# Bias loads on GpSimd's queue, a later request for the second tokens, a new order of the first norms, and another home for the residual, in a transformer block on one core

## The chip, the cores and the metric

The kernel runs on one core of one Trainium2 chip. The metric is the device time of one execution in microseconds (us), lower is better. A core has five engines that each work through their own queue of instructions in order: TensorE (PE in the profile; its weight loads are listed as PEld), VectorE (DVE), ScalarE (ACT), GpSimd (POOL) and SyncE (SP), which here only asks for DMA transfers. Engines wait for each other, and for transfers, through semaphores.

## The reference, cut to what matters

The input is 2048 tokens of 1024 features, all float32. The block is a layer norm and attention with a residual, then a layer norm and a gated feed-forward net with a residual:

```python
x = x + attn(layernorm(x), wq, bq, wk, bk, wv, bv)   # wl is not used for the result
x = x + ffn(layernorm(x), w1, w2, w3)

# attn: q, k, v = h @ w.T + b, seen as (token, 32 heads, 32);
scores  = einsum("bshd,bstd->bsht", q, k) / sqrt(32)  # 32 x 32 for each token: heads against heads
context = einsum("bsht,bstd->bshd", softmax(scores), v)

# ffn: w1, w2 (2752 x 1024) and w3 (1024 x 2752) are first quantized to 16 levels and back,
# in blocks of 64 that are scaled by the block's largest magnitude
y = (silu(h @ dq1.T) * (h @ dq2.T)) @ dq3.T
```

## The kernel before, in words

**Tiling.** Tokens lie in 16 tiles of 128. The three projections work on pairs of tiles, p = 0 to 7. Two token tiles by two halves of the features make a matrix of 2 by 2 blocks, and the weights are cut into 2 by 2 blocks too, so a pair's product is made with seven block products in place of eight (`products`, L352). Their left sides are the four blocks A11, A12, A21, A22 and four sums of these (`three` L398, `fourth` L403); their right sides are B11, B12, B21, B22 and four differences T1 to T4. The seven products come in a written order: B11, T3, T2, B21, T1, B22, T4. After the second and each later one `fill(n)` is called, with n = 7, 6, 2, 5, 3, 4 in turn, and does other work.

**Sweeps.** Three sweeps over the pairs follow each other: queries, keys, values. In the queries' sweep the tokens are loaded (`load_x` L458), normed (`normed` L329: statistics on VectorE, the power of -1/2 on GpSimd, the subtraction and scaling on VectorE), transposed on TensorE for the next pair (L486, four transposes into one PSUM tile `pt`, four such tiles per pair, three `pt` buffers), and copied out twice by ScalarE: L489 into A for the queries and keys, L490 into V, with another order of the tokens, for the values. Both A and V are stored to DRAM and read again in the later sweeps. The weights' differences T1 to T4 for queries are made once at the start (L519 to L534, L570); those for keys and values are made in eight chunks (`weight_chunk` L538), one per pair, and stored. A pair ends with `qk_T` (L411), which turns the two results to heads and adds the bias. The keys' sweep makes the scores and the softmax beside its products; the values' sweep makes the context, adds it to the tokens (`residual` L684), stores the sum to DRAM (x1d, L693), norms it (L337) and transposes it for the feed-forward part (`keep_T` L723), with four differences (L745) that go to DRAM through buffers `xU`.

**Background.** A generator, `background` (L219), works on the feed-forward weights all along: load a block of weights, take the largest magnitudes (`absmax` L200, with 16 small multiplications on ScalarE at L195), then 15 steps that build the level of each element. Twelve of these steps are a pair of a ScalarE instruction (L242, into one of two buffers `sg`) and a VectorE instruction (L243), which reads it. Another 16 multiplications at L195 (or one at L254 later) undo the scale. `advance(n)` takes n steps of the generator; `finish` (L147) transposes a finished block on TensorE (`ptw`, L161), copies it out (L162) and stores it (wd, L180). `scaled` (L192) is what issues the rows at L195.

**Feed-forward part.** From about 783 us on, gate and up products run with seven products again (`Unit` L912), and the down products are copied out at L1037 and added into x1d in DRAM by GpSimd's accumulating DMAs (L1039).

**What sets the order.** TensorE's instructions run as written (L283). For the other engines a planner orders what is ready, so a step of the background can be put before or behind a copy that TensorE needs. `tc.issue_after(i)` puts what it encloses behind i in the queue of i's own engine; it is an order of issue and no wait for i's end. SyncE asks for the transfers in the planner's order, and a request waits there until its own conditions hold, with all behind it.

**The opening.** SyncE asks for token tile 0 in two halves and tile 1, then for the weight blocks B11, B22, the one that becomes T1, and B21 (L503 to L508). ScalarE asks for the three biases in four pieces each (L509, `load_bias` L323). TensorE does 16 transposes of the identity. VectorE makes the statistics of tile 0, those of tile 1, and then both norms; their GpSimd parts are kept in order through `opening`. The first products follow; the second tiles (2 and 3) are loaded at the top of the loop (L564).

Of the kernel before, what the change touches and what calls it, by code (L numbers as in the profile page):

```python
# [12 lines left out]
FP = mybir.dt.float32  # L13
AF = mybir.ActivationFunctionType
ALU = mybir.AluOpType
# [3 lines left out]
P = 128  # L19
# [50 lines left out]
def preln_block_kernel(  # L70
# [39 lines left out]
    fs = ctx.enter_context(tc.tile_pool(name="fs", bufs=2))  # L110
    hook = {"scale": "ACT"}

    def mean_var(pool, src, dst):
        st = pool.tile([P, 2, 6], FP, tag="st", name="st")
        for j in range(2):
            nc.vector.bn_stats(st[:, j, :], src[:, ts(j, 512)])
        nc.vector.bn_aggr(dst, st.rearrange("p a b -> p (a b)"))
# [73 lines left out]

    def scaled(dst, src, by, nb):  # L192

        for n in range(nb):
            nc.scalar.mul(dst[:, ts(n, BLOCK)], src[:, ts(n, BLOCK)], by[:, n : n + 1])  # L195

    def width(kind, c):
        return KC * min(P, F - c * P) if kind == "3" else E
# [61 lines left out]
    def advance(n):  # L260
        for _ in range(n):
            next(bg, None)
# [57 lines left out]
        src = block(m, *RAW[name]) if name in RAW else wtD[m, int(name[1])]  # L320
        nc.sync.dma_start(new_w(name), src)

    def load_bias(b, nm):  # L323
        t = wpool.tile([P, 32], FP, tag=nm, name=nm)
        for g in range(4):
            nc.scalar.dma_start(t[g * 32 : (g + 1) * 32, :], b)
        return t

    def normed(src, dst, order=None):  # L329
        mv = small.tile([P, 2], FP, tag="mv", name="mv")  # L330
        rs = small.tile([P, 1], FP, tag="rs", name="rs")
        mean_var(small, src, mv)
        with tc.issue_after(order["last"]) if order else nullcontext():
            order_end = inv_std(rs, mv[:, 1:2])
        if order is not None:
            order["last"] = order_end.ins
        done = nc.vector.tensor_scalar(dst, src, mv[:, 0:1], rs, ALU.subtract, ALU.mult)  # L337
        hook["normed"] = done.ins
        return dst
# [114 lines left out]
    ps_t = sweep.enter_context(tc.tile_pool(name="ps_t", bufs=3, space=PSUM, side="right"))  # L454

    xt = {}

    def load_x(i):  # L458
        xt[i] = work.tile([P, E], FP, tag="x", name="xt", bufs=2)
        for n in range(2 if i == 0 else 1):  # L460
            cols = ts(n, TB) if i == 0 else slice(None)
            nc.sync.dma_start(xt[i][:, cols], xf[ts(i, P), cols])

    opening = {}

    def normed_x(i):
        xn = work.tile([P, E], FP, tag="xn", name="xn", bufs=2)
        return normed(xt.pop(i), xn, opening if i < 2 else None)

    class Inputs:  # L470

# [10 lines left out]
        def transposes(self, j):  # L482
            for half in range(2):
                pt = ps_t.tile([P, 4, P], FP, tag="pt", name="pt")
                for k in range(4):
                    nc.tensor.transpose(pt[:, k, :], self.xn[j][:, ts(4 * half + k, P)], ident)  # L486
                n = (SA11, SA12, SA21, SA22)[2 * j + half]
                a, v = (self.a21, self.v21) if n == SA21 else (self.A[:, n], self.V[:, n])
                nc.scalar.copy(a, pt)  # L489
                nc.scalar.copy(  # L490
                    v.rearrange("p k (c m) -> p k c m", c=4),
                    pt.rearrange("p k (m c) -> p k c m", c=4),
                )

        def finished(self):
# [10 lines left out]
    load_W("q", "B22")  # L506
    nc.sync.dma_start(new_w("T1"), block("q", 0, 1))
    load_W("q", "B21")  # L508
    qb_sb, kb_sb, vb_sb = (load_bias(b, nm) for b, nm in ((qb, "qb"), (kb, "kb"), (vb, "vb")))  # L509

    warm = ps_t.tile([P, 4, P], FP, tag="pt", name="warm")
    for _ in range(16):
# [3 lines left out]
    nxt.transposes(1)  # L516
    b12 = W["T1"]
    new_w("T3"), new_w("T2"), new_w("T4")
    with tc.issue_after(three(nxt.A, nxt.a21).ins):  # L519
        for n in range(2):  # L520
            k = slice(2 * n, 2 * n + 2)
            t3 = nc.vector.tensor_tensor(  # L522
                W["T3"][:, k], W["B22"][:, k], b12[:, k], ALU.subtract
            )
# [35 lines left out]
    for p in range(NP):  # L560
        more = p + 1 < NP
        now = nxt
        if more:
            load_x(2 * p + 2)  # L564
            load_x(2 * p + 3)
            with nullcontext() if p else tc.issue_after(opened):
                nxt = Inputs(p + 1)
            if p == 0:
                with tc.issue_after(hook["normed"]):
                    nc.vector.tensor_tensor(W["T4"], W["B21"], W["T2"], ALU.subtract)  # L570

        def fill(n):
            if n in (7, 3):
                flush(1)
            if n == 5 and more:
                nxt.transposes(0)
                nxt.transposes(1)
            with nullcontext() if p else tc.issue_after(opened):
                advance(0 if n == 5 else 1)

        cs = products(now.A, fill, (lambda name: None) if more else next_W("k"), ps_t)
        flush(1)
        if more:
            nxt.finished()
        for j in range(2):
            t = work.tile([P, 32, NH], FP, tag="qd", name="qd", bufs=2)
            qk_T(t, cs[j], qb_sb)
            nc.sync.dma_start(qD[2 * p + j], t)
        with nullcontext() if p else tc.issue_after(opened):
            now.finished_v()  # L590
        weight_chunk("kv"[p // 4], p % 4)
        advance(2)
        if p == NP - 2:
            first = load_A(opD, 0)
    sweep.close()


    sweep, sweep_at = ExitStack(), ExitStack()
    work = sweep.enter_context(
        tc.tile_pool(name="workk", bufs=1, side="right", reuse_waits="tile")  # L600
# [83 lines left out]
    def residual(i, at, x1):  # L684

        cx = work.tile([P, E], FP, tag="cx", name="cx")
        nc.vector.transpose(
            cx.rearrange("p (h d) -> p d h", d=D),
            at[:, :, 0:256].rearrange("p c (s d) -> p d s c", d=D),
        )  # L690
        nc.vector.tensor_tensor(x1, x1, cx, ALU.add)
        for n in range(2):
            nc.sync.dma_start(x1d[i][n], x1[:, ts(n, TB)])  # L693
        return normed(x1, x1)

    ops = {}

# [25 lines left out]
    def keep_T(i, x1n):  # L723

        t = work.tile([P, 2, 4, P], FP, tag=f"xT{i % 2}", name="xT")
        for half in range(2):
            pt = bank("pt").rearrange("p (k t) -> p k t", t=P)
            for k in range(4):
                nc.tensor.transpose(pt[:, k, :], x1n[:, ts(4 * half + k, P)], ident)
            nc.scalar.copy(t[:, half], pt)  # L730
        cols = ts(i // 2 % 4, P)
        tbp = i // 8
        names = ("B11", "B21") if i % 2 == 0 else ("B12", "B22")
        for n in range(2):
            nc.sync.dma_start(xd[names[n], tbp][:, :, cols], t[:, n])
        if i % 2 == 0:
            even["t"] = t
            return
        b11, b21 = even["t"][:, 0], even["t"][:, 1]
        b12, b22 = t[:, 0], t[:, 1]  # L740
        u = {}
        for n in range(4):
            u[n + 1] = work.tile([P, 4, P], FP, tag="xU", name="xU", bufs=2)
            y, z = ((b12, b11), (b22, u.get(1)), (b22, b12), (b21, u.get(2)))[n]
            nc.vector.tensor_tensor(u[n + 1], y, z, ALU.subtract)  # L745
            nc.sync.dma_start(xd[f"T{n + 1}", tbp][:, :, cols], u[n + 1])
# [464 lines left out]
```

## Time and profile before

| | us |
|---|---|
| median of three runs | 2480.15 |
| lowest, highest | 2476.73, 2480.97 |
| the profiled execution | 2484.77 |
| its span, first to last instruction | 2483.0 |
| TensorE busy | 2389.2 (96% of the span) |
| VectorE busy | 1981.2 (80%) |
| ScalarE busy | 1610.2 (65%) |
| GpSimd busy | 278.4 (11%) |

The queries' sweep takes the span's first 240 us or so, the keys' goes to about 537, the values' to about 783. The page lists busy times, the groups of instructions by line, and who waited for whom. "Idle before" is the time that an engine stood still before a row, and the arrow names what ended it. Line numbers (L489) are those of the kernel before. A busy TensorE is not TensorE at its best: its granted clock, a column of the tables by stretches, is 0.5 in ten stretches of 3.4 or 6.8 us before 820 us, and 1.0 in most others.

### The profile page before, as it was taken

Reading aid. Unit: us, or ns where it says so; the run is one execution under the profiler, and the core shown is the slowest. Engines: PE = TensorE matmul, PEld = TensorE weight load, DVE = VectorE, ACT = ScalarE, POOL = GpSimd, SP = SyncE. Lnnn points to the kernel's source line nnn. Section 1 sums busy time; section 2 is a strip of 40 time slices with the busy share of each in tenths; the row PEclk is TensorE's granted clock in tenths of the full one; section 3 lists DMA queues with packets and bytes.
Section 4 is the critical chain, followed back from the end, with each engine's and each line's share of the span. In section 5 each row is a group of like instructions: output and inputs, shape, how many; then the busy total and the mean of one; then the engine's idle time right before and its main releaser. Section 6 shows DMA issues by size and latency. Waiting matters only on the chain.

```text
span 2483.0 us, 36752 instructions
## 1 busy us (share of the span) xinstructions
PE 2389.2 (96%) x14000; PEld 1117.1 (45%) x14000; DVE 1981.2 (80%) x2211; ACT 1610.2 (65%) x3267; POOL 278.4 (11%) x352
## 2 busy tenths in 40 slices
PE   7999999999899999999999999999999999999998
PEld 4444455545445444444444444444444444444433
DVE  8999688879988597889989899898998988871022
ACT  3566544344554278898887888889889798881200
POOL 0010000000000012030120301203012030020300
PEclk9999999999999999999999999999999999999999
DMA  8888543666669588384883948739577394872983
GB/s 310 301 295 339 214 154 125 228 221 216 198 234 317 196 299 172 126 183 156 310 186 114 185 163 289 181 140 183 165 280 173 132 206 159 278 159 88 173 310 122
DMA packets 179745, 513.90 MB, mean 207 GB/s; under 512 B 16176, under 2 KB 70448, under 8 KB 157168
## 3 DMA queue, kind: packets, MB, share of 16 engines
q1 hardware_dynamic: 138672, 438.08, 48.5%
q0 software_dynamic: 40320, 73.42, 18.4%
q8 instruction: 110, 1.80, 0.3%
q14 instruction: 67, 0.55, 0.1%
q10 hardware_dynamic: 576, 0.05, 0.0%
HBM read 283.69 MB, written 227.80 MB: 206 GB/s over the span
## 4 chain that ended last, share of the span: by engine, by line
issue 25%; ACT 13%; DVE 13%; PE 11%; DMA 6%; POOL 1%; DVEq 0%; POOLq 0%; ACTq 0%
DVE r L243 8%; DMA x1d<-acc 5%; ACT sg L242 4%; PE z L343 4%; ACT wn L195 4%; ACT acc L1037 2%; ACT r L195 2%; PE z L1024 2%; PE q L343 2%; PE po L1104 1%; POOL x1d L1039 1%; PE po L1115 1%; PE y L1024 1%; PE rr L343 1%; ACT wop L162 1%
## 5 line engine op out<-in xcount | busy, mean ns | idle before, releaser
L243 DVE SCALAR_TENSOR_TENSOR r<-sg,r 128x1024 f32<-128x1024 f32 x780 | 945.3, 1213 | 104.1 <-ACT sg L242 72.7
L242 ACT ACTIVATE sg<-wn 128x1024 f32<-128x1024 f32 x780 | 812.6, 1053 | 309.6 <-DVE r L243 294.0
L1039 POOL DMA_DIRECT2D x1d<-acc x280 | 243.0, 887 | 1282.1 <-ACT acc L1037 1138.4
L343 PE MATMUL z<-xB,w 128*128 128x512 f32 x720 | 324.6, 599 | 5.6 <-ACT u L944 3.8
L343 PE MATMUL z<-xT,w 128*128 128x512 f32 x656 | 298.1, 597 | 4.6 <-ACT u L937 4.3
L343 PE MATMUL q<-xT,w 128*128 128x512 f32 x656 | 291.6, 592 | 0.0
L195 ACT ACTIVATE wn<-wn,rc 128x64 f32<-128x64 f32 x1032 | 267.5, 341 | 19.1 <-DVE rc L215 19.1
L1024 PE MATMUL z<-w,h 128*128 128x512 f32 x496 | 233.6, 599 | 9.4 <-ACT acc L1037 6.5
L343 PEld LDWEIGHTS z<-xB,w 128*128 128x128 f32 x720 | 134.6, 191 | 173.6 <-issue 153.0
L343 PEld LDWEIGHTS z<-xT,w 128*128 128x128 f32 x656 | 122.4, 191 | 154.4 <-issue 137.0
L343 PEld LDWEIGHTS q<-xT,w 128*128 128x128 f32 x656 | 123.3, 190 | 149.5 <-issue 146.9
L343 PE MATMUL z<-wT,A 128*128 128x512 f32 x384 | 178.2, 607 | 2.9 <-ACT g L362 2.5
L343 PE MATMUL q<-wT,A 128*128 128x512 f32 x384 | 174.5, 598 | 2.5 <-DVE wT L522 2.5
L343 PE MATMUL z<-wB,A 128*128 128x512 f32 x320 | 153.9, 626 | 12.8 <-ACT u L362 12.8
L195 ACT ACTIVATE r<-r,am 128x64 f32<-128x64 f32 x608 | 154.8, 342 | 14.6 <-DVE r L243 14.3
L1024 PE MATMUL y<-w,h 128*128 128x512 f32 x320 | 150.4, 594 | 1.3 <-DVE h L1003 1.1
L343 PE MATMUL rr<-xB,w 128*128 128x512 f32 x328 | 147.5, 592 | 0.0
L1024 PEld LDWEIGHTS z<-w,h 128*128 128x128 f32 x496 | 92.1, 191 | 121.7 <-issue 96.7
L207 DVE TENSOR_REDUCE am<-wn 128x16 f32<-128x1024 f32 (+1 forms) x65 | 78.3, 1204 | 54.5 <-ACT r L195 54.2
L1037 ACT COPY acc<-z 128x512 f32<-128x512 f32 x160 | 92.9, 580 | 36.9 <-PE z L1024 26.3
L343 PEld LDWEIGHTS q<-wT,A 128*128 128x128 f32 x384 | 72.6, 192 | 90.5 <-issue 85.4
L343 PEld LDWEIGHTS z<-wT,A 128*128 128x128 f32 x384 | 71.5, 193 | 83.0 <-issue 78.1
(132 smaller groups left out, 2585.8 us busy)
## 6 DMA issues: line engine op xcount, KB each, us to landing
x1d<-acc POOLq DMA_DIRECT2D x280, 256.0 KB, 6.4
wd<-wop SPq DMA_DIRECT2D x31, 2048.0 KB, 7.5
w<-wd SPq DMA_DIRECT2D x41, 1280.0 KB, 7.8
wn<-in_w_dram SPq DMA_DIRECT2D x63, 512.0 KB, 5.0
xT<-xdT SPq DMA_DIRECT2D x28, 1024.0 KB, 9.2
xB<-xdB SPq DMA_DIRECT2D x24, 1024.0 KB, 9.0
w<-wd SPq DMA_DIRECT2D x42, 512.0 KB, 5.0
w<-wd SPq DMA_DIRECT2D x10, 1536.0 KB, 7.6
```

What stands on the lines that cost most here:

```text
L162: nc.scalar.copy(o[:q, first + half], pt[:q])
L195: nc.scalar.mul(dst[:, ts(n, BLOCK)], src[:, ts(n, BLOCK)], by[:, n : n + 1])
L207: nc.vector.tensor_reduce(am[:, :nb], v.rearrange("p (b e) -> p b e", e=BLOCK), AX.X, ALU.max, apply_absolute_value=True,)
L242: nc.scalar.activation(t, v, AF.Copy, bias=-edge * by, scale=by)
L243: nc.vector.scalar_tensor_tensor(r, t, code, r, ALU.min, ALU.max)
L343: nc.tensor.matmul(dst, w[:, k, :], xop[:, k, :], start=start and k == 0, stop=stop and k == 3, skip_group_check=True,)
L1024: nc.tensor.matmul(dst, side[n][:, ts(q, P)], w3T[g[2 * m]][:, W3[n]], start=start and m == 0, stop=stop and m == 1, skip_group_check=True,)
L1037: nc.scalar.copy(t, src)
L1039: nc.gpsimd.dma_start(x1d[8 * tbp + 2 * q + j][n], t, accum_op=ALU.add)
L1104: nc.tensor.matmul(po, hs[c][j][:, ts(q, P)], w3T[c][:, ts(n, 512)], start=(c == g[0]), stop=False, skip_group_check=True,)
L1115: nc.tensor.matmul(po, hs[NFULL][r, ts(q, P)], w3T[NFULL][r, ts(n, 512)], start=False, stop=True, skip_group_check=True,)
```

## The change: the order of the opening, the queue of the biases, and three buffers

- The twelve bias requests move from ScalarE's queue to GpSimd's. They stand behind the GpSimd part of tile 1's norm. The bias of the queries gets its buffer in the sweep's own pool.
- All of tile 1's norm on VectorE, statistics too, is queued behind the norm of tile 0.
- The request for tile 2 on SyncE now waits until `three` has ended on VectorE for the first pair (`opening["first"]`).
- In the queries' sweep, the small multiplications of `scaled` are queued on ScalarE behind the last copy into V that was written before them (`marked`, `behind`).
- In the first pair, `fill` takes no step of the background at n = 7, 6 and 2; these three steps come later.
- In `residual`, the sum of tokens and context is written over the context (`cx`, one buffer), stored from there, and the norm is written to `x1`. Before, the sum was written over the tokens, stored from there and normed in place.
- `xU` gets three buffers in place of two.

```diff
+    urgent = {"last": None, "rule": ()}
+
+    def marked(ins):
+        urgent["last"] = ins.ins
+
+    def behind(kind):
+        last = urgent["last"]
+        return tc.issue_after(last) if last and kind in urgent["rule"] else nullcontext()
...
     def scaled(dst, src, by, nb):
-        for n in range(nb):
-            nc.scalar.mul(dst[:, ts(n, BLOCK)], src[:, ts(n, BLOCK)], by[:, n : n + 1])
+        with behind("scale"):
+            for n in range(nb):
+                nc.scalar.mul(dst[:, ts(n, BLOCK)], src[:, ts(n, BLOCK)], by[:, n : n + 1])
...
-    def load_bias(b, nm):
-        t = wpool.tile([P, 32], FP, tag=nm, name=nm)
+    def load_bias(b, nm, pool):
+        t = pool.tile([P, 32], FP, tag=nm, name=nm)
         for g in range(4):
-            nc.scalar.dma_start(t[g * 32 : (g + 1) * 32, :], b)
+            nc.gpsimd.dma_start(t[g * 32 : (g + 1) * 32, :], b)
...
+    urgent["rule"] = ("scale",)          # back to () after the queries' sweep
...
-            nc.sync.dma_start(xt[i][:, cols], xf[ts(i, P), cols])
+            load = nc.sync.dma_start(xt[i][:, cols], xf[ts(i, P), cols])
+        if i == 2:
+            tc.add_manual_dep(
+                load.ins,
+                opening["first"].name,
+                mybir.DependencyInfo(
+                    mybir.DependencyClass.Sync, mybir.DependencyReason.DATA
+                ),
+                reason="the first weights come first",
+            )
...
-        return normed(xt.pop(i), xn, opening if i < 2 else None)
+        with tc.issue_after(hook["normed"]) if i == 1 else nullcontext():
+            return normed(xt.pop(i), xn, opening if i < 2 else None)
...
-                nc.scalar.copy(
-                    v.rearrange("p k (c m) -> p k c m", c=4),
-                    pt.rearrange("p k (m c) -> p k c m", c=4),
+                marked(
+                    nc.scalar.copy(
+                        v.rearrange("p k (c m) -> p k c m", c=4),
+                        pt.rearrange("p k (m c) -> p k c m", c=4),
+                    )
                 )
...
-    qb_sb, kb_sb, vb_sb = (load_bias(b, nm) for b, nm in ((qb, "qb"), (kb, "kb"), (vb, "vb")))
...
-    with tc.issue_after(three(nxt.A, nxt.a21).ins):
+    with tc.issue_after(opening["last"]):
+        qb_sb = load_bias(qb, "qb", work)
+        kb_sb = load_bias(kb, "kb", wpool)
+        vb_sb = load_bias(vb, "vb", wpool)
+    opening["first"] = three(nxt.A, nxt.a21).ins
+    with tc.issue_after(opening["first"]):
...
-                advance(0 if n == 5 else 1)
+                advance(0 if n == 5 or p == 0 and n in (7, 6, 2) else 1)
...
-        nc.vector.tensor_tensor(x1, x1, cx, ALU.add)
+        nc.vector.tensor_tensor(cx, x1, cx, ALU.add)
         for n in range(2):
-            nc.sync.dma_start(x1d[i][n], x1[:, ts(n, TB)])
-        return normed(x1, x1)
+            nc.sync.dma_start(x1d[i][n], cx[:, ts(n, TB)])
+        return normed(cx, x1)
...
-            u[n + 1] = work.tile([P, 4, P], FP, tag="xU", name="xU", bufs=2)
+            u[n + 1] = work.tile([P, 4, P], FP, tag="xU", name="xU", bufs=3)
```

More of the change, by code (lines that the diff above doesn't have):

```diff
@@ L595, in preln_block_kernel @@
     sweep.close()
+    urgent["rule"] = ()
     sweep, sweep_at = ExitStack(), ExitStack()
```

## The prediction, written before the changed kernel ran

> **What bounds the kernel now.** I read the page's busy times first, then the table by stretches over the first 240 us (the queries' sweep, where most edits lie), then who waited for whom, then the timeline around the longest waits.
>
> ```profile
> PE 2389.2 (96%) x14000; PEld 1117.1 (45%) x14000; DVE 1981.2 (80%) x2211; ACT 1610.2 (65%) x3267; POOL 278.4 (11%) x352
> ```
>
> TensorE is busy for 96%, so what can be won is its 94 us of idle time and the time at half clock. In the next view the columns are busy time and count of PE, PEld, DVE, ACT and POOL, then TensorE's granted clock, then the DMA engines' share and GB/s.
>
> ```profile
> 12.00:18.98 6.98, 4.47 (x12) 1.92 (x10) 3.36 (x5) 2.65 (x6) 0.00 (x0) 1.00 1.03 388
> 18.98:34.50 15.52, 15.52 (x32) 6.73 (x33) 15.07 (x20) 1.17 (x2) 1.48 (x4) 0.89 0.96 364
> 34.50:42.00 7.50, 1.49 (x13) 1.23 (x11) 7.12 (x12) 7.29 (x23) 0.00 (x0) 0.91 0.67 274
> 42.00:48.60 6.60, 6.57 (x12) 3.31 (x13) 6.60 (x9) 6.16 (x9) 0.00 (x0) 0.58 0.91 305
> 60.00:220.10 160.10, 152.35 (x432) 72.86 (x431) 155.02 (x215) 93.15 (x202) 13.81 (x20) 0.99 0.80 299
> 220.10:240.00 19.90, 19.90 (x49) 8.80 (x48) 19.43 (x23) 12.91 (x27) 0.00 (x0) 1.00 0.94 369
> ```
>
> Two things stand here. Up to 48.6 us TensorE loses 8.5 us by idling (2.5 and 6.0), and its clock is 0.50 for 20.2:23.6 and 40.7:47.5, where 10.2 us do 5.1 us of work. From 60 to 220 us VectorE is busy for 155 of 160 us: it has hardly more room than TensorE. Who TensorE waited for in the first 300 us (total, times, longest):
>
> ```profile
> PE pt L486 <- ACT V L490: 12.4, 4, 6.0
> PE q L343 <- DVE wT L522: 2.5, 1, 2.5
> PE z L343 <- ACT g L362: 2.5, 1, 2.5
> ```
>
> And on ScalarE's timeline, where the longest of these comes from:
>
> ```profile
> 34.71 0.59 ACT L362 COPY u<-z 128x512 f32<-128x512 f32 x1 [6.28 <-PE z L343]
> 35.19 3.93 ACT L195 ACTIVATE wn<-wn,rc 128x64 f32<-128x64 f32 x16
> 39.02 0.57 ACT L489 COPY A<-pt 128x512 f32<-128x512 f32 x1
> ...
> 41.39 0.59 ACT L490 COPY V<-pt 128x512 f32<-128x512 f32 x1
> ```
>
> Sixteen background scales stand between TensorE's transposes and the copies that free their PSUM tile. SyncE's own waits in the first 60 us:
>
> ```profile
> SPq L321 <- DMA wB<-in_wqT_dram: 3.5, 1, 3.5
> SPq L321 <- DMA kb<-in_kb_dram: 2.7, 1, 2.7
> SPq L321 <- DMA qb<-in_qb_dram: 1.8, 1, 1.8
> ```
>
> The weight requests were held back 8.0 us in all: the biases take turns at the same completion semaphores, so B11, asked for at 3.94, waited for a bias to land. T1's block, asked for at 7.47, landed at 17.6, and VectorE's first subtraction began at 17.70 after 2.67 us of idling.
>
> **The change part by part, the opening.** Without the biases all seven requests can be issued in a row (0.45 us each, by 4 us). Transfers land in order of request, T1's after 4 MB. At the 388 GB/s of 12.00:18.98 that is 10.8 us, from 2.0 us on: 12.8 us. At the 257 GB/s seen before 12 us it is 18.3 us, no gain. I take 13 to 14, since the row at 388 is the one in which biases are nearly gone. Then the next to be late is `three`: tile 0's norm moves from 8.09 to about 6.2, but tile 1's statistics (6.64) now wait for it, so tile 1's norm stays near 9.6. ScalarE is rid of twelve issues that kept it until 8.06, so its copies of tile 0 end some 2 us earlier, those of tile 1 about 0.9, and `three` ends near 14.4 in place of 15.03. T3's halves (1.18 each) are ready by 16.8, as TensorE ends B11's product (16.47). The idle 2.51 and the half clock after it (3.4 us, 1.7 lost) go; T2's second half, four subtractions of 1.2 later, costs back up to 0.3. Transposes of tiles 2 and 3: 34.51 less 3.9, about 30.6. Tile 2's request waits for `three`: asked for at 14.4 in place of 11.97, but two weight loads (0.5 MB each) pass it, so it lands at 19 to 21, where it landed at 21.6; nobody waits, since VectorE takes it up only after T2 (21.6 or so).
>
> The biases cost GpSimd 12 issues. The nearest row is L1039, 862 ns (up to 1218): 10.3 to 14.6 us from 9.5 on, so 20 to 24; GpSimd's next norm part is due at about 23.5. Ends: 0 and +1 us; I take 0, since the first user of a bias, L414, comes at 52.97. A rule of the Trainium skill speaks against this edit: SBUF — State Buffer, "A bandwidth-pool intuition that's wrong (but worth ruling out)", says a request that GpSimd issues, about 0.62 us alone, takes about 3.1 us beside a VectorE copy that holds the shared port. By that the twelve would end at 47 us and hold tile 2's norm by over 20. L1039 ran at 862 ns with VectorE busy for most of the time, so the sum goes by the row.
>
> **First pair's transposes.** The three skipped steps include the only one that puts L195 there. In the built order ScalarE now runs u4's copy and at once A, A, A21, V21, so the fourth transposes wait only for four copies, as at 72 us, where the wait was 1.36. The first pair ends earlier by 3.9, plus 6.04 - 1.36 = 4.7, plus the half clock 3.4: about 12 us, its last product at 40 in place of 52.07. There VectorE is late next. Its instructions up to that pair's L394 lose 8.4 us by median durations, most of it six code steps, and it begins T3 some 3 us earlier; as it then waits for ScalarE's copies, I put L394 at 42.5 for 52.38.
>
> **Pairs two to seven.** The skipped steps come back here. In the built order of VectorE, 45 code steps lie ahead of the seventh L394 (220.1 us) where 47 did, so over these six pairs VectorE has four steps more, 5 us, and was full. Its whole work to that point falls by 2.6 us by median durations; idle time that can go is 2.7 in the opening and up to 5 in 60:220. So the gain there is 2.6 + 2.7 = 5.3 to 10.3, whatever TensorE could do; I take 7. TensorE's own waits there hardly change: five of the six pairs now have the order A, A, A21, V21 (7 us), where the waits for V and AV without the first made 12.4 + 1.4 - 6.0 = 7.8. So VectorE decides.
>
> **Keys.** No edit here, but the background is out of step with the products: in the first two pairs 2.46 and 1.09 us of waits for ScalarE's copies and 6.8 us at clock 0.50 (3.4 lost) can vanish. In the built order 17 scales and a sign step precede the first u4, so I take half: -3; ends 0 and -7.
>
> **Values.** VectorE's waits from 530 to 870 us:
>
> ```profile
> DVE xU L745 <- DMA xdT<-xU: 11.2, 6, 4.0
> DVE x L337 <- DMA x1d<-x: 11.1, 5, 5.7
> ```
>
> The norm no longer waits for its own store, and the third `xU` takes most of the other. `cx` must now wait for the store before it is written again: pairs of stores and the next L687 lie 3 to 6 us apart at the tightest (stored by 767 to 768, written at 771.0), so 0 to +2. But who waited for VectorE? TensorE's longest waits there are for u4:
>
> ```profile
> 617.70 0.57 ACT L362 COPY u<-z 128x512 f32<-128x512 f32 x1
> 624.29 1.06 ACT L242 ACTIVATE sg<-wn 128x1024 f32<-128x1024 f32 x1 [6.03 <-DVE r L243]
> ...
> 627.91 0.57 ACT L362 COPY u<-z 128x512 f32<-128x512 f32 x1
> ```
>
> Three sign steps stand ahead of the copy and each needs VectorE to free `sg`. In the built order three pairs of the values' sweep still have this (sign steps between u2 and u4: 3, 4 and 3; before 3, 2 and 3, which cost 4.27, 3.29 and 4.13). What can go are the waits after 770 us, 8 us with three stretches at half clock (5.1 lost). I take -3 of these 13; ends +6 (one u4 stall more, 4.3 and 1.7 of clock) and -9.
>
> **Feed-forward part.** Its waits (some 30 us, 11.8 for `acc`) are a matter of where the background's rows fall; the built order has as many rows ahead of the critical copies as before. 0, with +-4.
>
> Sum: -7 - 3 - 3 = -13. The profiled execution took 2484.77 (span 2483.0), so 2471.8; it stood 4.6 above the median of the runs, so the median becomes 2467.
>
> **Rivals.** A: VectorE takes it back. If passes two to seven are as full as 155 of 160 says and the u4 copies there wait for sign steps, the first pair's 12 us shrink to 3, and keys and values shift without a gain: 2477. For it: 99.03 us busy in 100:200. Against it: the 2.7 us in the opening are VectorE's own.
>
> B, slower: the pattern at 617 us in the queries' sweep. There u4 stands ahead of the transposes' copies, and in the built order pairs two to seven all have two to four sign steps between u2 and u4, while VectorE is full. At 4.3 and 1.7 us each, less the 1.4 already counted, that is 4.6 a pair: all six cost 28 and end at 2495. It decides from four pairs on (18.4, more than 13 + 5). Against it: 100.67 had three sign steps and cost 2.59 with no loss of clock.
>
> C, more: the idle and half-clock stretches of keys and values after 260 us go too: -7 and -9 with -9 for queries, 2455.
>
> D: T1's block lands late anyway (18 us): the opening's 3.9 stay away, VectorE's gain falls to 3, sum -9: 2471, inside the forecast.
>
> **How the numbers follow.** Forecast (D with it) 0.55, own range 2460 to 2474; C 0.17; A 0.14; B 0.14. What a measurement can tell from no change is 0.2%, 5 us: under 2475.2 is faster, over 2485.1 slower. Faster is forecast and C, 0.72; same is A, 0.14; slower is B, 0.14. The range 2453 to 2484 takes in C and A and leaves B out.
>
> **What would show it.** T1's subtraction begins by 15 us with no wait over 1 us; no clock of 0.50 from 20 to 48 us; L195 after the copies into V; the first pair's L394 near 42.5 and the seventh's near 213; no L337 wait for a store. I am wrong if T1 still lands after 17 us, if GpSimd's issues take 3 us each and tile 2's norm is late, or if TensorE's waits for L362 and L490 in 50:220 exceed 15 us.

## The result, and the profile after

The changed kernel takes 2501.42 us (median of five runs, 2500.15 to 2504.92), the kernel before 2480.97 in the same comparison (2476.73 to 2483.29): a ratio of 1.0084, with the interval 1.0072 to 1.0097. It is slower, where 2467 was forecast. Its profiled execution took 2503.82 us (span 2502.0), 19.0 more than the span before; the medians lie 20.5 apart.

The changed kernel's lines are those of before plus 11 or 12 near the top (L180 is L191, L343 is L355, L362 is L374, L195 is L207), plus 23 or 24 in the queries (L486 is L509, L490 is L514), plus 30 further down (L818 is L848, L1024 is L1054). First the busy times on the page of the changed kernel:

```profile
PE 2388.8 (95%) x14000; PEld 1115.6 (45%) x14000; DVE 1984.7 (79%) x2211; ACT 1612.9 (64%) x3267; POOL 282.1 (11%) x364
```

No engine is busy for more than 3.7 us longer than before, and TensorE's busy time is the same within 0.4 us: the 19 us are idle time of TensorE (113.2 us for 93.8). The table by stretches (busy time and count of PE, PEld, DVE, ACT and POOL, then TensorE's clock, the DMA share and GB/s) shows that the queries' sweep, which the prediction looked at most, did get better:

```profile
8.00:12.00 4.00, 0.87 (x5) 0.79 (x5) 2.12 (x4) 1.76 (x4) 2.50 (x5) 0.53 1.04 382
12.00:18.98 6.98, 6.68 (x17) 3.34 (x16) 4.42 (x6) 2.64 (x5) 4.62 (x10) 0.78 1.06 389
18.98:34.50 15.52, 14.67 (x43) 6.62 (x41) 15.06 (x22) 2.94 (x6) 1.49 (x4) 1.00 0.98 375
60.00:220.10 160.10, 148.61 (x421) 71.10 (x419) 155.53 (x214) 92.90 (x202) 10.69 (x20) 0.98 0.80 303
```

The half clock from 20 to 24 us has gone, and so has that from 41 to 47. The one in 8 to 15 us is not new: in the kernel before, the 16 transposes at 8.90 us took 3.67 us, 0.23 each, where twelve at 34.51 took 1.47, 0.12 each, so TensorE was at half pace there too, although its row says 1.00; and before_late (an experiment below), whose opening is that of before, shows 0.50 from 7.6 to 14.4. From 60 to 220 us VectorE is as full as before. The first pair's copies now stand as predicted, with the scales (L207) behind them, in the timeline of the changed kernel:

```profile
32.73 0.59 ACT L374 COPY u<-z 128x512 f32<-128x512 f32 x1 [6.28 <-PE z L355]
33.21 1.57 ACT L512 COPY A<-pt 128x512 f32<-128x512 f32 x3
34.64 0.63 ACT L514 COPY V<-pt 128x512 f32<-128x512 f32 x1
...
43.93 3.94 ACT L207 ACTIVATE wn<-wn,rc 128x64 f32<-128x64 f32 x16
```

The loss is elsewhere. From 780 us on, who TensorE waited for (total, times, longest), in the changed kernel:

```profile
PE z L1054 <- ACT acc L1067: 13.8, 13, 2.3
PE z L1054 <- DMA w<-wd: 9.2, 1, 9.2
```

and in the kernel before, the same rows:

```profile
PE z L1024 <- ACT acc L1037: 11.8, 11, 2.2
...
PE z L1024 <- DMA w<-wd: 2.9, 1, 2.9
```

The second row is one event: TensorE needs the last large block of quantized w3, number 18, which the background has made and stored (L191) and SyncE loads again (L848). In the changed kernel's timeline:

```profile
2157.73 0.32 SPq L191 DMA_DIRECT2D wd<-wop  x1
2166.46 0.32 SPq L848 DMA_DIRECT2D w<-wd  x1
2172.49 4.43 PE L1054 MATMUL z<-w,h 128*128 128x512 f32 x6 [9.22 <-DMA w<-wd]
```

and before:

```profile
2140.39 0.32 SPq L180 DMA_DIRECT2D wd<-wop  x1
2148.81 0.32 SPq L818 DMA_DIRECT2D w<-wd  x1
2152.61 3.77 PE L1024 MATMUL z<-w,h 128*128 128x512 f32 x5 [2.90 <-DMA w<-wd]
```

The store is issued 17.3 us later, though TensorE was only 12.7 us behind at the last mark ahead of it (unit 35 in the count below). The block's load then landed 6.0 us after it was asked for, in place of 3.8; two other loads (L839, L840) had been asked for about 4 us ahead of it, but that they slowed it was not tested.

Where the 19.0 us came in, at marks on TensorE that both traces have (the start of a pair's last product, T4; in a feed-forward unit the start of its product with B21; units are counted from 1):

| mark | before, us | after, difference | in this stage |
|---|---|---|---|
| first pair of the queries | 48.6 | -9.4 | -9.4 |
| last pair of the queries | 240.3 | -4.4 | +5.0 |
| second pair of the keys | 301.7 | -1.0 | +3.4 |
| last pair of the keys | 497.4 | +0.7 | +1.7 |
| last pair of the values | 777.8 | +3.7 | +3.0 |
| first feed-forward unit | 842.5 | +6.5 | +2.8 |
| unit 32 | 2052.1 | +12.5 | +6.0 |
| unit 36 | 2211.4 | +20.3 | +7.8 |
| end | 2483.0 | +19.0 | -1.3 |

Such marks of single executions scatter by 2 to 3 us, as runs show in which nothing was edited up to a mark. The keys' last products end near 501 us; the 537 us given above for the end of the keys is the end of the values' first pair, in which the last scores are still made.

### The profile page after: what moved, and what is told of

It reads as the page before. It is cut to its first block, busy times and chain, and to the rows that moved or that the text cites. A ratio compares the mean times of both kernels' runs of the same rounds, so it can differ in the third digit from the quotient of the medians.

```text
span 2502.0 us, 36764 instructions
## 1 busy us (share of the span) xinstructions
PE 2388.8 (95%) x14000; PEld 1115.6 (45%) x14000; DVE 1984.7 (79%) x2211; ACT 1612.9 (64%) x3267; POOL 282.1 (11%) x364
## 4 chain that ended last, share of the span: by engine, by line
issue 23%; PE 17%; DVE 17%; ACT 12%; DMA 5%; POOL 2%; DVEq 0%; POOLq 0%; ACTq 0%
DVE r L255 10%; PE z L355 7%; DMA x1d<-acc 5%; ACT sg L254 4%; ACT wn L207 3%; PE q L355 3%; ACT acc L1067 2%; ACT r L207 2%; POOL x1d L1069 2%; PE z L1054 2%; PE po L1134 1%; PE rr L355 1%; PE y L1054 1%; PE cx L455 1%; PE po L1145 1%
## 5 line engine op out<-in xcount | busy, mean ns | idle before, releaser
L355 PE MATMUL z<-xB,w 128*128 128x512 f32 x720 | 324.8, 599 | 5.8 <-ACT u L974 2.1
L355 PE MATMUL z<-xT,w 128*128 128x512 f32 x656 | 296.6, 595 | 7.6 <-ACT u L967 5.7
L355 PE MATMUL q<-xT,w 128*128 128x512 f32 x656 | 291.3, 592 | 0.0
L207 ACT ACTIVATE wn<-wn,rc 128x64 f32<-128x64 f32 x1032 | 267.4, 343 | 34.0 <-DVE rc L227 34.0
L1054 PE MATMUL z<-w,h 128*128 128x512 f32 x496 | 235.8, 603 | 18.6 <-ACT acc L1067 9.2
L355 PEld LDWEIGHTS z<-xB,w 128*128 128x128 f32 x720 | 134.6, 191 | 172.8 <-issue 151.7
L355 PEld LDWEIGHTS z<-xT,w 128*128 128x128 f32 x656 | 121.7, 190 | 157.1 <-issue 137.0
L355 PEld LDWEIGHTS q<-xT,w 128*128 128x128 f32 x656 | 123.2, 190 | 149.0 <-issue 146.4
L355 PE MATMUL z<-wT,A 128*128 128x512 f32 x384 | 180.2, 613 | 6.1 <-ACT u L374 3.3
L355 PE MATMUL q<-wT,A 128*128 128x512 f32 x384 | 172.9, 593 | 0.3 <-DVE wT L551 0.3
L355 PE MATMUL z<-wB,A 128*128 128x512 f32 x320 | 152.6, 622 | 13.9 <-ACT u L374 13.9
L207 ACT ACTIVATE r<-r,am 128x64 f32<-128x64 f32 x608 | 154.9, 345 | 12.4 <-DVE r L255 12.2
L1054 PE MATMUL y<-w,h 128*128 128x512 f32 x320 | 151.6, 599 | 1.3 <-DVE h L1033 1.0
L1054 PEld LDWEIGHTS z<-w,h 128*128 128x128 f32 x496 | 92.6, 192 | 131.8 <-issue 99.1
L355 PE MATMUL rr<-xB,w 128*128 128x512 f32 x328 | 147.5, 592 | 0.0
L355 PEld LDWEIGHTS z<-wT,A 128*128 128x128 f32 x384 | 72.0, 194 | 88.4 <-issue 79.0
L970 DVE TENSOR_TENSOR g<-g,rr 128x512 f32<-128x512 f32 x41 | 27.9, 681 | 105.1 <-PE rr L355 105.1
```

The lines of the kernel that those rows point to most:

```text
L355: nc.tensor.matmul(dst, w[:, k, :], xop[:, k, :], start=start and k == 0, stop=stop and k == 3, skip_group_check=True,)
L970: nc.vector.tensor_tensor(self.g0, self.g0, r, ALU.add)
L1054: nc.tensor.matmul(dst, side[n][:, ts(q, P)], w3T[g[2 * m]][:, W3[n]], start=start and m == 0, stop=stop and m == 1, skip_group_check=True,)
```

## The experiments

Three theories. Theory 1, the lag: the three skipped steps are never made up, so the background stays three steps late to the end, and the end pays. Theory 2, the phase: the background's rows only fall at other places, and any shift, early or late, costs or wins by chance. Theory 3, the home: the residual over the context, or the third `xU`, costs. Each row below is against runs of the kernel before on the same chip; "w3 wait" is TensorE's longest wait for that last block.

| run | median (range), us | ratio, 95% | w3 wait |
|---|---|---|---|
| changed kernel | 2501.4 (2500.2 to 2504.9) | 1.0084, 1.0072 to 1.0097 | 9.2 |
| before_skip | 2499.1 (2494.8 to 2500.2) | 1.0065, 1.0050 to 1.0080 | 9.7 |
| before_late | 2498.2 (2494.7 to 2501.8) | 1.0070, 1.0055 to 1.0085 | 9.1 |
| before_late6 | 2492.7 (2486.4 to 2500.5) | 1.0049, 1.0031 to 1.0068 | 7.9 |
| after_pay | 2490.3 (2486.1 to 2492.8) | 1.0031, 1.0018 to 1.0044 | 2.6 |
| after_noskip | 2489.4 (2475.9 to 2491.8) | 1.0028, 1.0015 to 1.0042 | 2.3 |
| after_pay_norule | 2484.5 (2478.9 to 2487.2) | 1.0012, 1.0003 to 1.0021 | 2.8 |
| before_res | 2483.8 (2480.7 to 2487.5) | 1.0010, 1.0001 to 1.0020 | 2.8 |
| before_pay | 2483.7 (2480.9 to 2488.9) | 1.0012, 1.0002 to 1.0022 | 2.4 |
| after_pay6_norule | 2481.8 (2478.9 to 2485.0) | 0.9999, 0.9989 to 1.0008 | none |
| after_open | 2480.8 (2475.8 to 2484.7) | 0.9998, 0.9988 to 1.0008 | 3.1 |
| before_pay6 | 2478.6 (2476.5 to 2480.5) | 0.9992, 0.9983 to 1.0001 | 0.4 |
| before_early | 2477.6 (2473.5 to 2481.5) | 0.9986, 0.9976 to 0.9996 | none |

The medians of the kernel before were 2480.97 beside the changed kernel, 2481.24 beside before_skip, before_res, after_noskip and after_pay, 2481.12 beside before_late, before_early, before_pay and after_pay_norule, and 2480.86 beside before_late6, after_open, before_pay6 and after_pay6_norule.

**The skip alone, in the kernel before.**

```diff
-                advance(0 if n == 5 else 1)
+                advance(0 if n == 5 or p == 0 and n in (7, 6, 2) else 1)
```

> The kernel before with nothing but the three steps skipped. Theory 1: the first pair gains about 6 to 9 us and the wait for w3 near 2150 us grows from 2.9 to about 9: the total is the same as before within 5 us. Theory 2: 2475 to 2505 with losses in keys and feed-forward part spread as in the changed kernel. Theory 3: no loss in the values' sweep, so faster, about 2474.

2499.1 us, 17.9 over before. Theory 1 had the wait for w3 right (9.7) and the total wrong by more than 12 us; only the wide range of theory 2 took it in. Alone, this one line costs nearly as much as the whole change, and it brings nearly all of the first pair's gain too: that pair ends 8.0 us earlier here, 9.4 in the changed kernel. By the end of the queries 2.9 of the 8.0 are left.

**The changed kernel without the skip.**

```diff
-                advance(0 if n == 5 or p == 0 and n in (7, 6, 2) else 1)
+                advance(0 if n == 5 else 1)
```

> The changed kernel with the three background steps of the first pair put back. Theory 1: the wait for w3 near 2172 us is again about 3 us, which gains 8, but the first pair's stall behind the 16 scales comes back (6 us and 3 of clock), so about 2500 with the loss in another place. Theory 2: 2490 to 2510, spread. Theory 3: the feed-forward part and the total as in the changed kernel, plus the first pair's 8, about 2509.

2489.4, just under what theory 2 gave and further under the others: 12.0 of the 20.5 us go, and the w3 wait is back at 2.3. So 8 us of the loss are there without the skip. With the 17.9 of the skip alone that makes 26, more than the 20.5: the parts overlap, and no exact share can be given to either.

**The skip kept, its three steps given back in the keys' sweep.**

```diff
             parts.append(attend(2 * p + j, qd[j], t))
-        advance(2)
+        advance(3 if p in (3, 4, 5) else 2)
```

> The changed kernel with the three skipped background steps given back in the keys' sweep (one more in each of pairs 3, 4 and 5), where VectorE idles. Theory 1, the background is late at the end: the wait for the last w3 block near 2172 us falls from 9.2 to about 3 us with its half clock, total about 2494. Theory 2, the background's rows only fall elsewhere and the cost is spread by chance: the wait may go, but the total moves by up to 10 us either way, with no rule. Theory 3, the residual's new home costs: the wait and the total stay at about 2501.

2490.3, 11.1 less than the changed kernel. With the steps back, the feed-forward part has the length of before again, unit 1 to unit 36 within 0.4 us. The stages that had 2.8, 6.0 and 7.8 us in the table have -1.2, 0.1 and 0.3 here.

**The residual's home and the third buffer alone, in the kernel before** (with the bias of the queries in the sweep's pool, for the room).

```diff
-        nc.vector.tensor_tensor(x1, x1, cx, ALU.add)
+        nc.vector.tensor_tensor(cx, x1, cx, ALU.add)
...
-            nc.sync.dma_start(x1d[i][n], x1[:, ts(n, TB)])
-        return normed(x1, x1)
+            nc.sync.dma_start(x1d[i][n], cx[:, ts(n, TB)])
+        return normed(cx, x1)
...
-            u[n + 1] = work.tile([P, 4, P], FP, tag="xU", name="xU", bufs=2)
+            u[n + 1] = work.tile([P, 4, P], FP, tag="xU", name="xU", bufs=3)
```

> The kernel before with nothing but the residual's new home, the third xU buffer and the query bias in the sweep's pool (which makes the room). Theories 1 and 2: VectorE's 22 us of waits for stores mostly go, TensorE gains 0 to 5 us up to 846 us, the wait for w3 stays 2.9, total 2474 to 2483. Theory 3: the values' sweep and what follows lose 5 us or more, 2486 or more.

2483.8, +0.10% (0.01 to 0.20). What VectorE waited for from 530 to 870 us in this kernel:

```profile
DVE co L383 <- ACT u L362: 9.8, 4, 4.7
DVE x L337 <- POOL rs L121: 9.3, 13, 0.9
...
DVE xU L746 <- DMA xdT<-xU: 5.5, 2, 4.7
```

The 11.1 us of L337's wait for its own store are gone and the buffer's wait is halved, and the time did not fall (0.8 us above what theories 1 and 2 gave): VectorE only waits for the next thing. Theory 3 falls as the cause of the 20 us, and the prediction's gain with it.

**Lag or phase: three steps fewer, and three more, in the kernel before.** Nothing else is edited. The late one:

```diff
-        advance(2)
+        advance(1 if p in (3, 4, 5) else 2)
```

> The kernel before with three background steps fewer, taken from the keys' sweep (one fewer in pairs 3, 4 and 5), nothing else: no edit in the queries' sweep. Theory 1, a background that is three steps late costs at the end whatever the place it was made late: the wait for w3 near 2150 us is 8 to 10 us in place of 2.9, the stretch with it 8 us longer, the total 2491 to 2497. Theory 2, only the chance of where rows fall: the wait stays under 5 us and the total lies anywhere within 2475 to 2490.

The early one:

```diff
-        advance(2)
+        advance(3 if p in (3, 4, 5) else 2)
```

> The kernel before with three background steps more in the keys' sweep (pairs 3, 4 and 5), nothing else. Theory 1: the wait for w3 near 2150 us goes from 2.9 to 0 with its half clock, total 2475 to 2478. Theory 2: no rule, 2475 to 2495.

Late: 2498.2, +17.1. Early: 2477.6, -3.5. Three late steps cost as much as the skip, though they are taken out in another sweep, and three early ones cost nothing. By stage, the late kernel loses 6.5 us between the last values' pair and the first feed-forward unit and 7.7 from unit 32 to unit 36 (the w3 wait, with its half clock); before_skip loses 6.2 and 7.9 in the same two. (Between units 1 and 32 the two lose 3.6 and 2.1, near the scatter; the late one wins 3.7 in the values' sweep.) The first place, in the waits of before_late from 774 to 846 us:

```profile
PE pt L729 <- DVE x L337: 7.6, 1, 7.6
```

and in its timeline:

```profile
823.31 1.20 DVE L691 TENSOR_TENSOR x<-x,cx 128x1024 f32<-128x1024 f32 x1
824.43 1.21 DVE L243 SCALAR_TENSOR_TENSOR r<-sg,r 128x1024 f32<-128x1024 f32 x1
...
827.35 1.21 DVE L243 SCALAR_TENSOR_TENSOR r<-sg,r 128x1024 f32<-128x1024 f32 x1
...
829.15 2.55 DVE L243 SCALAR_TENSOR_TENSOR r<-sg,r 128x1024 f32<-128x1024 f32 x2
831.61 0.81 DVE L337 TENSOR_SCALAR x<-x,mv,rs 128x1024 f32<-128x1024 f32 x1
832.57 1.94 PE L729 MATMUL pt<-ident,x 128*128 128x128 f32 x8 [7.55 <-DVE x L337]
```

In the values' sweep's last tile the norm that TensorE waits for stands among code steps of the background (L243), of which four fall here between the residual (L691) and the norm (L337). Before, none did at this last tile: the background was at its scales and maxima there. This first place is a matter of phase (in the changed kernel, with its other order, it cost 2.8, not 6); the second is a deadline.

**The skip in the kernel before, its steps given back.** The two edits shown above together, the skip and `advance(3 if p in (3, 4, 5) else 2)`.

> The kernel before with the three steps skipped in the first pair and given back in the keys' sweep; no other edit of the change. Theory 1: the first pair's gain (8 us, of which 3 are left after the queries) stays and the 16 us that the skip cost elsewhere go: 2476 to 2481, the feed-forward part as in the kernel before within 1 us. Theory 2: 2485 to 2500 as with the skip alone.

2483.7. The first pair ends 10.0 us earlier, the queries 5.6, the keys 3.7, the whole 2.3 in the profiled execution and nothing by the median (+0.12%), 2.7 us above what theory 1 gave. So even with no lag the first pair's gain does not reach the end.

**The rule on the scales.** The kernel after_pay without it:

```diff
-    urgent["rule"] = ("scale",)
```

> The changed kernel with the steps given back and without the rule for the scales. The changed kernel with the steps given back still loses some 3.5 us in the first two keys' pairs and 5 in the queries' later pairs. If the rule does it (scales piled up behind the copies into V), these come back: 2480 to 2485. If the opening's edits do it, 2488 to 2492 as with the rule.

2484.5, against 2490.3 with the rule; the intervals of the two ratios just touch (1.0021 and 1.0018). One place shows in the first two keys' pairs. TensorE's waits in after_pay, 236 to 301 us:

```profile
PE z L355 <- ACT u L374: 4.1, 2, 3.3
...
PE z L355 <- ACT g L374: 1.8, 1, 1.8
```

and without the rule, 236 to 298 us:

```profile
PE sc L441 <- DMA ql<-qD: 2.9, 1, 2.9
PE z L355 <- ACT u L374: 0.6, 2, 0.4
```

The stage is 3.5 us longer than before with the rule, and no longer without it. The keys' later pairs give 2.3 of it back, and at the end the two profiled executions lie 2.2 apart where the medians lie 5.8 apart; where the rest sits was not found.

**The opening alone.** The changed kernel with the skip, the rule, the residual's edits and the third buffer undone:

```diff
-    urgent["rule"] = ("scale",)
...
-                advance(0 if n == 5 or p == 0 and n in (7, 6, 2) else 1)
+                advance(0 if n == 5 else 1)
...
-        nc.vector.tensor_tensor(cx, x1, cx, ALU.add)
+        nc.vector.tensor_tensor(x1, x1, cx, ALU.add)
```

> The changed kernel with only its opening left: the bias queue, the order of the first norms and the later request for tile 2. The skip, the rule on the scales, the residual's home and the third xU are as before. If the skip was what moved the first pair, the first pair ends 1 to 3 us earlier than before's 48.6 and the time is 2478 to 2483. If the opening is worth what the prediction gave it (3.9 us at the first pair), the time is 2475 to 2478.

2480.8, a ratio of 0.9998: nothing. Its first pair ends 2.9 us earlier than in the trace of before (45.8 us), and 1.1 to 2.2 earlier than in the four other traces with the opening of before and no skip (46.9 to 48.0); the fourth ends 1.5 later, the queries 1.3 earlier.

**Twice the lag: six steps fewer in the kernel before.**

```diff
-        advance(2)
+        advance(1 if p in (1, 2, 3, 4, 5, 6) else 2)
```

> The kernel before with six background steps fewer in the keys' sweep (one after pairs 1 to 6 in place of two), twice the lag of the run with three fewer (2498.2, wait for the last w3 block 9.1 us). If the lag is carried to the end, TensorE's wait for the last w3 block grows by another 6 us to about 15 us and the time goes to 2507 to 2515. If three late steps cost by bringing rows into a bad order once, and not by their number, the wait stays near 9 us and the time near 2498.

2492.7, outside both expectations: 11.8 us, where three steps cost 17.1, with 7.9 us for the last block and 2.6 for an earlier one, and 7.0 before the first unit. The two intervals overlap (1.0031 to 1.0068, 1.0055 to 1.0085), so that six cost less than three is not shown; that they don't cost twice as much is.

```profile
PE z L1024 <- DMA w<-wd: 10.5, 2, 7.9
```

The lag itself is carried to the end, and in full. From the last mark on TensorE ahead of each, the 29 stores of blocks behind 850 us are issued later than before by this much (median of the 29):

| run | steps | all 29, us | block 18, us |
|---|---|---|---|
| before_early | 3 early | -4.3 | -2.5 |
| after_pay, after_noskip | none | 0.0 | 0.0, 0.3 |
| changed kernel, before_skip, before_late | 3 late | 4.7 | 4.7 |
| before_late6 | 6 late | 9.4 | 3.8 |

Single blocks lie on both sides of the median (-1.7 to 12.1 with three late steps), but the three kernels with three late steps agree at each block within 1.2 us. Six steps late is twice as late; only block 18 is not, and the written program says why. A block is given out in pieces between products, and where a unit asks for one that isn't stored, the missing pieces are forced in front of the request (`until`, L264). For block 18 the kernel before, the early one and after_pay force none, the changed kernel, before_skip and before_late one piece, before_late6 two; no other block is forced in any of them. The request then stands directly behind the store, and the block's way to DRAM and back lies open. So the forcing bounds how late that one block can be (here 3.8 to 4.7 us), and with it what the lag costs there. That is theory 1 for the lag and for this deadline. What the lag costs on the way (7.0 before the first unit) hangs on which rows fall there, as theory 2 has it.

**Being ahead, with the shorter first pair.** The kernel before with the skip and six steps given back:

```diff
-                advance(0 if n == 5 else 1)
+                advance(0 if n == 5 or p == 0 and n in (7, 6, 2) else 1)
...
-        advance(2)
+        advance(3 if p in (1, 2, 3, 4, 5, 6) else 2)
```

> The kernel before with the three steps skipped in the first pair and six more in the keys' sweep (three after pairs 1 to 6 in place of two), so that the background is three steps ahead of the kernel before from then on. If being ahead is worth what the run with three steps more showed (3.5 us), the time is 2483.7 - 3.5, about 2480, and TensorE has no wait for the last w3 block. If the background can use no more lead, it stays at 2484; if the first pair's 8 us and the lead add up, 2470 to 2474.

2478.6, 0.9992 (0.9983 to 1.0001): as the lead alone would give. The first pair's 7.4 us are spent by the end of the keys (+2.4 there).

**The same lead with all of the change but the rule.** The changed kernel without `urgent["rule"] = ("scale",)`, and with the last edit above.

> The changed kernel without the rule on the scales and with six more steps in the keys' sweep, three steps ahead of the kernel before from then on. By the lead's 3.5 us, 2484.5 - 3.5, about 2481; without a use for the lead 2484.5; if opening, third xU and lead add up, under 2475, faster than both kernels.

2481.8, 0.9999. The parts do not add up to a gain. The one kernel that is faster than both by its interval is the kernel before with three background steps more, by 0.14%, which is under what the prediction took for measurable.

## Why the prediction was wrong

**The step that failed is "The skipped steps come back here", with the feed-forward part's "0, with +-4" that rests on it.** The prediction counted the three steps' return on VectorE in the queries' pairs and then let the background go on as before. On VectorE its count was near: 55 code steps had run by the last pair of the queries where 57 had, and 75 by the second of the keys in both. But the number of steps in each later place is written down, so the background stays three steps behind in the program, and in the feed-forward part its blocks are stored 4.7 us late at the median, to the last one. The stages behind the values measured +15.3 (6.5 - 3.7 is 2.8, then 6.0, 7.8 and -1.3), where the term was 0. The 7.8 is the wait for block 18 with its half clock, and the 2.8 holds a wait of 2.7 for a norm (1.0 before). The 6.0 between units 1 and 32 (3.1 of idle time, and two stretches of half clock) were not followed to one row: before_skip and before_late have 2.1 and 3.6 there, and 0.1 is left where the steps are given back. The sign could have been read from the profile of before: TensorE already waited 2.9 us for block 18, so there was no slack at that deadline. The prediction listed the feed-forward's waits for `acc` and passed this row over. Done alone, the three late steps cost 17.1 or 17.9 us in the kernel before.

**T1's block, "13 to 14".** It landed at 16.5, inside the stated bounds and short of the 17 that was to refute it; rival D had 18. The sign that was to show it, a first subtraction by 15 us with no wait over 1 us, did not come: it began at 16.64, after 1.26. In the changed kernel's timeline:

```profile
7.81 1.29 DVE L127 BATCH_NORM_STATS2 st<-xt 128x6 f32<-128x512 f32 x2 [0.85 <-DMA xt<-in_x_dram]
...
11.24 1.94 PE L509 MATMUL pt<-ident,xn 128*128 128x128 f32 x8 [3.13 <-DVE xn L349]
...
16.64 2.36 DVE L551 TENSOR_TENSOR wT<-wB,wT 128x1024 f32<-128x1024 f32 x2 [1.26 <-DMA wT<-in_wqT_dram]
...
17.91 3.70 PE L355 MATMUL q<-wT,A 128*128 128x512 f32 x8 [0.30 <-DVE wT L551]
```

Six requests were issued by 3.7 us and the seventh was begun at 3.75, as said, and they landed in the order of request (B22 at 13.8, T1's block at 16.5, B21 at 19.4). But "T1's after 4 MB" was wrong. By 16.54 us the core had moved 5.0 MB (165, 268, 382 and 389 GB/s over 4, 4, 4 and 4.54 us), where the two token tiles and the three weight blocks up to T1's make 4.2 (1 MB is 10^6 bytes here): 0.8 MB of what was asked for later had moved along with it. One after another, at these rates, T1's block would have been in by about 14.4. Token tile 1 was hit as well. Its statistics began at 7.81, against 6.64 before, and TensorE waited 2.0 and 3.1 us for the two norms, where it had waited 3.83 for both. T1's product began at 17.91, against 18.98. The opening's 3.9 us came out as 1.1 to 2.9 in after_open at the first pair and 0.0 at the end, by the medians.

**Bias issues on GpSimd, "0".** Right. The row L1039 was a high price:

```profile
10.20 2.50 POOL L338 DMA_DIRECT2D qb<-in_qb_dram  x4
...
12.69 1.97 POOL L338 DMA_DIRECT2D kb<-in_kb_dram  x4
...
16.02 1.97 POOL L338 DMA_DIRECT2D vb<-in_vb_dram  x4 [1.36 <-DMA qb<-in_qb_dram]
```

Twelve issues took 6.4 us, 0.54 each, and were over by 18.0, eight us before GpSimd's next norm part (26.37). VectorE was busy for 6.5 of the 11 us in 8:18.98. The first of the twelve took 1.01 us, from 10.20 to 11.21, while VectorE subtracted and scaled (10.28 to 11.09); the others took 0.50 to 0.53, beside VectorE's subtractions too. The 3.1 us for one that the Trainium skill has beside a VectorE copy (SBUF — State Buffer, "A bandwidth-pool intuition that's wrong (but worth ruling out)") did not occur here; no run here has such a copy beside them.

**First pair, "about 12 us", L394 "at 42.5".** The pair ended 9.4 earlier, and its L394 (L406 after) ran at 43.0. Scales behind the copies, a wait of 1.32 for 1.36: the mechanism was right, and so was "no clock of 0.50 from 20 to 48 us". The copies gave the 4.7 us as said; the opening gave 2.0 in place of 3.9 (the second tiles' transposes began at 32.53, before at 34.51), and the half clock 2.7 in place of 3.4.

**Pairs two to seven, "I take 7".** 4.4, under the range 5.3 to 10.3; the seventh L394 ran at 216.5, where 213 was said. VectorE took the gain back more fully than the term allowed. Between the first and the last of the queries' marks, before and after (columns as in the table by stretches):

```profile
48.60:240.30 191.70, 183.96 (x509) 87.10 (x508) 186.12 (x252) 109.07 (x234) 15.28 (x24) 0.99 0.81 306
39.30:235.90 196.60, 185.11 (x505) 87.27 (x504) 191.05 (x258) 117.67 (x255) 13.37 (x24) 0.98 0.82 310
```

VectorE is idle for 5.6 us in both, and the 4.9 us more time are work. It was busy 7.8 us less in the first pair, and 2.0, 3.0 and 2.8 more up to the fourth pair, to the eighth and to the second of the keys. These add up to nearly the same 7.8. And the seven traces with the skip lose 4.4 to 6.4 us in this stretch, with the scales' rule and without it, the six edited ones without the skip -0.9 to 2.4. "TensorE's own waits there hardly change" was wrong, though: it waited 11.5 us for copies out of `pt` in 50:220, against 7.7 before, and had one more stretch of half clock. That these waits only pass on VectorE's load was not tested. 11.5 is below the 15 that would have spoken for rival B:

```profile
PE pt L509 <- ACT V L514: 10.5, 5, 2.8
PE pt L509 <- ACT AV L514: 1.0, 1, 1.0
```

B, the rival that ended at 2495 as slower, had its place in the queries and is not what happened. A's mechanism (VectorE takes it back) did, and took 5.0 us by the end of the queries; 28.4 were lost in all behind the first pair.

**Keys, "I take half: -3".** Measured +5.1, outside its ends (0 and -7). The waits for ScalarE's copies in the first two pairs (3.6 before) did not vanish: 5.9 us with the rule on, 0.6 without it. The 3.4 of these two pairs go with the rule (after_pay_norule); the 1.7 of the later ones are within the scatter.

**Values, -3.** Measured +3.0, inside its ends. The norm's wait for its store went as said. TensorE waited three times for u4 copies, 13.1 us in all, as counted from the built order. The waits that went freed VectorE and not TensorE: before_res, which has this edit alone, gained nothing.

**Sum.** -4.4 + 5.1 + 3.0 + 15.3 is +19.0, for -7 - 3 - 3 + 0. Three of the four terms were off by 2.6 to 8.1 us, and the fourth by 15.3, the largest part of the 32 us between forecast and result.

## What to carry to other kernels

Where a producer runs beside the main work at a fixed number of steps for each place, a step taken out has to be put back in the text before the next deadline, or everything it makes is late from there on; so look for the last consumer of its product, and for the slack that it has. A wait of a few us for a product of the producer, even a single one, says that the slack is zero. How late the producer is and what this costs are two things: here twice the lag cost no more, and at the deadline the request forces what is missing. And a gain on TensorE counts only as far as the next full engine lets it through: compare that engine's busy time up to a mark well behind the edit, not the end of the edited pair.

## What the runs showed that was not expected

- Issuing all large requests earlier made the first small one later: token tile 1's statistics began at 7.81 us instead of 6.64, at 268 GB/s in 4:8 against 304. Requests of one queue overlapped: they landed in order, but 0.8 MB of later ones had moved by the time that T1's block was in.
- A store followed by a load of the same data costs the sum of both: from the issue of the store of block 18 to the product that reads it, 14.8 us in the changed kernel and 12.2 before. The load was issued 8.7 and 8.4 us after the store, when the store had landed.
- Six late steps cost no more (11.8 us) than three (17.1), with a wide scatter from run to run (2486.4 to 2500.5), though the blocks were stored twice as late (9.4 for 4.7 us at the median).
